# Two indirect transfers at a time: a wait ahead of each gather, add and store of a two-layer graph network

## The chip, the cores and the metric

One core of a Trainium2 chip runs the kernel. The metric is device time in microseconds, the median of several executions. Three executions of the kernel before took 1087.29, 1087.72 and 1098.17 us; the median is 1087.72 us. The profile is of one more execution.

## The reference

Input `x` has 32 batches of 512 nodes with 512 features, `adj` is a 512 x 512 matrix with few nonzero entries. Both layers normalise each row, take the positive part, mix and add the result to `x`:

```python
h = jnp.maximum(_layernorm(x, axis=-1), 0.0)
x = x + einsum(adj, h) @ weight + bias                 # layer 0: adj mixes the nodes
h = jnp.maximum(_layernorm(x, axis=-1), 0.0)
q, k, v = h @ Wq + bq, h @ Wk + bk, h @ Wv + bv        # layer 1: 8 heads
scores = q k^T / sqrt(64) + (1 - adj) * -1e9
x = x + softmax(scores) v @ Wo + bo
```

Where the penalty is so large that one neighbour takes the whole softmax, the attention of a row is a copy of one other row. The kernel establishes on the chip that this holds for its inputs, and then layer 1 is a product of the rows that are pointed at with `Wv Wo`, followed by a gather.

## The kernel before, in words

A prologue multiplies the weights, finds the neighbour of each row and decides on the path. `single_path` then handles one batch per round. Batches 0 to 4 run in the order of the input; beside them a `Plan` works out a new order of the nodes, in which the nonzero entries of `adj` fall into few blocks. From batch 5 (`FIRST`) on, `phase(range(FIRST, B + 1), True)` runs the regrouped loop (`sparse` is true), in which the rows of `x` are fetched and stored in the new order by indirect transfers. All indirect transfers are issued by GpSimd (POOL), one after the other, and their queue is q0 in the profile; plain transfers are issued by SyncE and go to q1.

A round `b` has 21 steps. `put(batch, step, f)` files a piece of work under a step; TensorE runs `layer0(b)` with steps 0 to 6, then `aggregate(b + 1)` (`spread`, L608 to L614) with steps 7 to 13, then `layer1(b - 1)` with steps 14 to 20. The order is written out by hand (`manual_schedule`); each engine runs its instructions in this order and waits on semaphores for data. The indirect transfers of a round, in POOL's order, each of 128 rows of 2 KB:

- `load_x(b + 2)`, step 0: four gathers of `x` into one of five buffers (`x<-in_x_dram,xi`, L462). A buffer is free once the stores of the batch before in it have landed.
- `load_g(b + 2)`, step 4: three gathers of extra rows into a single buffer (`at<-in_x_dram,gi`, L462). It is free once ScalarE has normalised the rows of the batch before out of it (`more_relu`, L933). ScalarE takes the statistics of the new rows in steps 13 to 18 (`more_stats`, L920).
- `finish(b - 2)`, step 7: four gathers that add the rows of layer 1 from memory onto `x` (`x<-z,pplace`, L462). They need the transfers `z<-zr` that SyncE issued after `put_z` (a transpose on VectorE, L718).
- `layer1` begins with a memset on POOL (L713) that clears the unused columns of `zs`. VectorE's transpose of `zs` in step 20 (`put_z`, L718) reads them.
- `store(b - 2)`, step 14: four scatters into the output (`out_dram<-x,xi`, L479), each followed by a small memset (L482).

In the first three rounds of the loop some of these are plain transfers or absent, since batches up to 5 are still in the input's order. The last rounds gather the last batches' layer 1 into buffers of their own (`fetch`, `get_all`).

Of the kernel before, what the change touches and what calls it, by code (L numbers as in the profile page):

```python
# [408 lines left out]
def single_path(ctx: ExitStack, tc: tile.TileContext, x, adj, out, kept, room):  # L409
    nc = tc.nc  # L410
    B, N, D = x.shape
# [28 lines left out]
    X, H0, PUT = {0: xs[0], 1: xs[1]}, {0: hs[0], 1: hs[1]}, {}  # L440
# [7 lines left out]
    def phase(batches, sparse):  # L448
        with ExitStack() as inner:
            small = inner.enter_context(tc.tile_pool(name="small", bufs=4))  # L450
            ps_m = inner.enter_context(tc.tile_pool(name="ps_m", bufs=6, space=PSUM))
            ps_t = inner.enter_context(tc.tile_pool(name="ps_t", bufs=2, space=PSUM))
            run_phase(batches, sparse, small, ps_m, ps_t)

    def run_phase(batches, sparse, small, ps_m, ps_t):
        ordered = folded and (sparse or batches[0] == 0)

        def natural(b):
            return not ordered or b <= FIRST

        def gather(dst, rows, at, **more):
            return nc.gpsimd.indirect_dma_start(out=dst, out_offset=None, in_=rows,  # L462
                                                in_offset=bass.IndirectOffsetOnAxis(ap=at, axis=0), **more)

        def load_x(b):
            X[b] = xs[b % 5]
            for c in range(C):
                if natural(b):
                    nc.sync.dma_start(X[b][:, c, :], x[b, c * P:(c + 1) * P, :])
                else:  # L470
                    gather(X[b][:, c, :], x_rows, plan.xi[:, b, c:c + 1])
# [3 lines left out]
        def store_rows(b, c, eng):  # L475
            if natural(b):
                eng.dma_start(out[b, c * P:(c + 1) * P, :], X[b][:, c, :])
                return
            stored = nc.gpsimd.indirect_dma_start(  # L479
                out=out_rows, out_offset=bass.IndirectOffsetOnAxis(ap=plan.xi[:, b, c:c + 1], axis=0),  # L480
                in_=X[b][:, c, :], in_offset=None)
            nc.gpsimd.memset(gap, 0.0)  # L482
            for other_rows in stored_rows:
                tc.declare_no_dep(stored.ins, other_rows.ins, reason="other rows")
            stored_rows.append(stored)

        def store(b):
            for c in range(C):
                store_rows(b, c, nc.sync)
# [84 lines left out]
        def look_up(table):  # L574
            for c in range(C):
                gather(place[:, c:c + 1], table, idx[:, c, 0:1])
# [44 lines left out]
        def load_g(b):  # L621
            for j in range(3):
                gather(plan.gx[:, j, :], x_rows, plan.gi[:, b, j:j + 1])
# [55 lines left out]
        def layer1_rows(b):  # L679
            for r in range(C):  # L680
                bank = ps_m.tile([P, D], F32, name="mm")
                for d in range(DC):
                    if d == 2 and r + 1 < C:
                        transpose_all(r + 1)
                    nc.tensor.matmul(bank, hs[1][:, d, r * P:(r + 1) * P], wvo[:, d, :], start=(d == 0),  # L685
                                     stop=(d == DC - 1))
                x_r = X[b][:, r, :].rearrange("p (q c e) -> p q c e", q=4, c=4)
                nc.vector.tensor_add(x_r, bank.rearrange("p (c q e) -> p q c e", q=4, c=4), x_r)
                store_rows(b, r, nc.sync)
                for i in range(2):  # L690
                    add_z(B - 3 + r // 2, 2 * (r % 2) + i, nc.sync if r < 2 else nc.scalar)
# [44 lines left out]
        def add_z(b, c, eng):  # L736
            nc.vector.tensor_add(X[b][:, c, :], late_z[b][:, c, :], X[b][:, c, :])
            store_rows(b, c, eng)
# [16 lines left out]
                                    pattern=[[1, P]], channel_multiplier=-1)  # L755
        last = []
        for b in batches:
            todo = [[] for _ in range(21)]

            def put(batch, step, f, *args):  # L760
# [805 lines left out]
```

## Time and profile before

| | before |
|---|---|
| median of the runs | 1087.72 us |
| profiled execution | 1089.15 us, span 1087.4 us |
| TensorE busy | 1011.2 us (93%) |
| VectorE busy | 810.1 us (74%) |
| ScalarE busy | 581.0 us (53%) |
| GpSimd busy | 564.2 us (52%) |
| indirect transfers of x: gathers, adds, stores | 104, 92, 104 |
| gathers of extra rows | 78 |
| time of the packets of q0 / q1, share of 16 engines | 45.4% / 30.0% |

A busy time on POOL is the time in which it makes a transfer's descriptors (1555 ns for an add, 948 to 1076 ns for the others), not the time until its data has landed. The page's list of DMA issues has no time to landing for indirect transfers; the chain of waits, and the semaphores' events, show some. An idle time stands before an instruction with what ended it: "issue" is none that the profile can name.

### The profile page before, as it was taken

What the parts mean: (1) busy time and instruction counts of PE and PEld (TensorE: products, weight loads), DVE (VectorE), ACT (ScalarE), POOL (GpSimd) and SP (SyncE); (2) the same over time, 40 slices, a digit from 0 to 9 for tenths busy, and PEclk for the clock granted to TensorE, in tenths of its full rate; (3) what the DMA queues carried; (4) which work ended last, traced back from release to release, by engine and by line L of the source; (5) the groups of instructions that cost most, each with busy time, mean ns of one, the idle gap of its engine ahead of it and who ended that gap; (6) DMA issues with size and microseconds to landing.
All of it is one profiled execution on the core that took longest, in us unless ns stands there. A gap on an engine that the chain in (4) does not pass through costs nothing.

```text
span 1087.4 us, 17059 instructions
## 1 busy us (share of the span) xinstructions
PE 1011.2 (93%) x5672; PEld 900.0 (83%) x5672; DVE 810.1 (74%) x1809; ACT 581.0 (53%) x1266; POOL 564.2 (52%) x659
## 2 busy tenths in 40 slices
PE   8999889978999889999999999999999998999993
PEld 7478778877898878999999988888889888999871
DVE  5897876857787658878777777778777776888762
ACT  3745345255555465566556556665555556666230
POOL 1023216646547435665575575555665565564326
PEclk9999999989899989999999999999999999999997
DMA  9244546968888768888888898988788787987654
GB/s 315 92 85 125 125 111 198 229 193 194 169 207 207 168 178 198 196 201 202 209 219 184 210 232 206 214 196 201 198 207 193 171 213 202 221 197 188 131 169 159
DMA packets 161314, 204.24 MB, mean 188 GB/s; under 512 B 17824, under 2 KB 105632, under 8 KB 161216
## 3 DMA queue, kind: packets, MB, share of 16 engines
q0 software_dynamic: 43984, 118.27, 45.4%
q1 hardware_dynamic: 115760, 83.37, 30.0%
q10 hardware_dynamic: 1472, 1.41, 0.4%
q8 instruction: 47, 0.77, 0.3%
q14 instruction: 51, 0.42, 0.1%
HBM read 120.66 MB, written 82.32 MB: 187 GB/s over the span
## 4 chain that ended last, share of the span: by engine, by line
PE 72%; ACT 4%; DVE 3%; issue 2%; POOL 2%; DMA 1%; another core or an unknown queue 1%; ACTq 0%; POOLq 0%; DVEq 0%
PE mm L495 51%; PE mm L611 11%; PE mm L614 6%; PE mm L608 2%; ACT zs L545 1%; POOL out_dram L479 1%; PE mm L685 1%; DVE st L361 1%; ACT h L379 1%; DMA x<-z,pplace 1%; DVE x L552 0%; DMA at<-in_x_dram,gi 0%; ACT h L394 0%; ACT yT L619 0%
## 5 line engine op out<-in xcount | busy, mean ns | idle before, releaser
L552 DVE TENSOR_TENSOR x<-mm,x 128x512 f32<-128x512 f32 x217 | 148.5, 685 | 130.2 <-PE mm L495 99.3
L379 ACT ACTIVATE h<-x,off,rstd 128x512 f32<-128x512 f32 x256 | 196.5, 807 | 7.8 <-DVE off L370 4.1
L365 ACT ACTIVATE rstd<-mv,eps 128x2 f32<-128x2 f32 (+1 forms) x91 | 26.6, 293 | 300.5 <-DVE mv L362 252.8
L495 PE MATMUL mm<-w_t,sel 128*128 128x256 f32 x744 | 176.1, 386 | 9.5 <-DVE x L552 9.4
L462 POOL DMA_INDIRECT x<-z,pplace x92 | 143.1, 1555 | 72.9 <-DMA z<-zr 37.4
L495 PEld LDWEIGHTS mm<-w_t,sel 128*128 128x128 f32 x744 | 142.1, 192 | 32.2 <-DVE x L552 12.7
L361 DVE BATCH_NORM_STATS2 st<-x 128x6 f32<-128x512 f32 x234 | 157.7, 674 | 1.1
L462 POOL DMA_INDIRECT at<-in_x_dram,gi x78 | 73.9, 948 | 162.0 <-ACT adjT L933 131.6
L495 PE MATMUL mm<-hTs,wvo_t 128*128 128x168 f32 x720 | 122.8, 317 | 32.3 <-ACT zs L545 31.0
L611 PE MATMUL mm<-ap,h 128*128 128x256 f32 x624 | 151.9, 380 | 0.0
L462 POOL DMA_INDIRECT x<-in_x_dram,xi x104 | 111.9, 1076 | 57.4 <-issue 27.1
L495 PEld LDWEIGHTS mm<-hTs,wvo_t 128*128 128x128 f32 x720 | 109.4, 196 | 38.6 <-ACT zs L545 37.3
L479 POOL DMA_INDIRECT out_dram<-x,xi x104 | 108.2, 1040 | 31.2 <-issue 22.0
L545 ACT ACTIVATE zs<-mm,cvo_c 128x168 f32<-128x168 f32 x240 | 82.8, 399 | 68.9 <-PE mm L495 50.9
L611 PEld LDWEIGHTS mm<-ap,h 128*128 128x128 f32 x624 | 110.6, 191 | 10.7
L495 PE MATMUL mm<-w_s,yT 128*128 128x256 f32 x496 | 118.5, 382 | 0.8 <-ACT zs L545 0.8
L495 PEld LDWEIGHTS mm<-w_s,yT 128*128 128x128 f32 x496 | 93.6, 192 | 12.7 <-ACT zs L545 1.0
L614 PEld LDWEIGHTS mm<-ag,adjT 128*128 128x128 f32 x624 | 86.0, 191 | 5.4
L614 PE MATMUL mm<-ag,adjT 128*128 128x128 f32 x624 | 86.4, 275 | 0.0
L586 DVE TENSOR_TENSOR x<-x,b_r 128x512 f32<-128x512 f32 x124 | 84.1, 679 | 0.0
L495 PE MATMUL mm<-hT,wvo 128*128 128x168 f32 x480 | 81.2, 314 | 0.0
L619 ACT COPY yT<-mm 128x512 f32<-128x512 f32 x104 | 59.8, 575 | 38.9 <-PE mm L614 30.3
(314 smaller groups left out, 1703.0 us busy)
## 6 DMA issues: line engine op xcount, KB each, us to landing
hc<-hs SPq DMA_DIRECT2D x124, 176.0 KB
z<-zr SPq DMA_DIRECT2D x120, 96.0 KB
z<-zr SPq DMA_DIRECT2D x120, 80.0 KB
hs<-h SPq DMA_DIRECT2D x50, 192.0 KB
hs<-h SPq DMA_DIRECT2D x50, 160.0 KB
out_dram<-x SPq DMA_DIRECT2D x24, 256.0 KB
x<-in_x_dram SPq DMA_DIRECT2D x16, 256.0 KB
x<-in_x_dram,xi POOLq DMA_INDIRECT x104
```

Source lines behind the costliest of these rows:

```text
L361: self.nc.vector.bn_stats(st, self.src[:, self.chunks[i], :])
L365: self.nc.scalar.activation(self.rstd[:, 0:len(self.chunks)], self.mv[:, :, 1], AF.Sqrt, bias=self.eps)
L379: self.nc.scalar.activation(dst, src, AF.Relu, bias=self.off[:, i:i + 1], scale=self.rstd[:, i:i + 1])
L462: return nc.gpsimd.indirect_dma_start(out=dst, out_offset=None, in_=rows, in_offset=bass.IndirectOffsetOnAxis(ap=at, axis=0), **more)
L479: stored = nc.gpsimd.indirect_dma_start(out=out_rows, out_offset=bass.IndirectOffsetOnAxis(ap=plan.xi[:, b, c:c + 1], axis=0), in_=X[b][:, ...
L495: nc.tensor.matmul(bank[:, m, 0:half], lhs[:, k, m * P:(m + 1) * P], rhs[:, k, :], start=(first and m == 0 and k == 0), stop=(k == 1), ski ...
L545: nc.scalar.activation(dst[:, m, :], bank[:, m, :], AF.Identity, bias=cvo_c[:, 2 * i + m:2 * i + m + 1])
L552: nc.vector.tensor_add(dst, bank, dst)
L586: nc.vector.tensor_add(X[b][:, c, :], X[b][:, c, :], b0_r)
L611: nc.tensor.matmul(two(bank, j), H0[b][:, j, cols], two(plan.ap[:, j, :], j), start=False, stop=False, skip_group_check=True)
L614: nc.tensor.matmul(bank[:, j * P:(j + 1) * P], extra[:, j - 1, cols], plan.ag[:, j - 1, j * P:(j + 1) * P], start=False, stop=(j == C - 1) ...
L619: nc.scalar.copy(yT[:, d, :], bank)
```

## The change

Each indirect transfer that `gather` and `store_rows` issue in the regrouped loop is passed through `paced`. It makes the transfer depend on the one issued two before it, as a dependence on data: POOL waits until that one has landed. `pacing[0]` turns this off for rounds 30 to 32. The transfers, their order and their data stay as they are.

```diff
+        moved, pacing = [], [True]
+
+        def paced(move):
+            if sparse and pacing[0]:
+                if len(moved) > 1:
+                    tc.add_manual_dep(move.ins, moved[-2].ins.name, mybir.DependencyInfo(
+                        mybir.DependencyClass.Sync, mybir.DependencyReason.DATA), reason="two at a time")
+                moved.append(move)
+            return move
+
         def gather(dst, rows, at, **more):
-            return nc.gpsimd.indirect_dma_start(out=dst, out_offset=None, in_=rows,
-                                                in_offset=bass.IndirectOffsetOnAxis(ap=at, axis=0), **more)
+            return paced(nc.gpsimd.indirect_dma_start(out=dst, out_offset=None, in_=rows,
+                                                      in_offset=bass.IndirectOffsetOnAxis(ap=at, axis=0), **more))
...
-            stored = nc.gpsimd.indirect_dma_start(
+            stored = paced(nc.gpsimd.indirect_dma_start(
                 out=out_rows, out_offset=bass.IndirectOffsetOnAxis(ap=plan.xi[:, b, c:c + 1], axis=0),
-                in_=X[b][:, c, :], in_offset=None)
+                in_=X[b][:, c, :], in_offset=None))
...
         for b in batches:
+            pacing[0] = b < B - 2
             todo = [[] for _ in range(21)]
```

## The prediction

> **What bounds the kernel now.** I read the busy shares on the page first, then the chain that ended last, then the waits inside the regrouped loop (412 to 984 us), then one round of that loop on the timeline.
>
> ```profile
> PE 1011.2 (93%) x5672; PEld 900.0 (83%) x5672; DVE 810.1 (74%) x1809; ACT 581.0 (53%) x1266; POOL 564.2 (52%) x659
> ...
> q0 software_dynamic: 43984, 118.27, 45.4%
> ...
> PE 72%; ACT 4%; DVE 3%; issue 2%; POOL 2%; DMA 1%; another core or an unknown queue 1%; ACTq 0%; POOLq 0%; DVEq 0%
> ```
>
> TensorE sets the pace: 93% busy, 72% of the chain. POOL, which issues every indirect transfer (queue q0), is half idle, and DMA is 1% of the chain. The waits of POOL in the loop (who waits for whom: us in total, times, longest) say why it is idle:
>
> ```profile
> POOL at L462 <- ACT adjT L933: 98.8, 21, 9.2
> ...
> POOL x L462 <- DMA z<-zr: 26.7, 10, 4.0
> ...
> POOL x L462 <- DMA out_dram<-x,xi: 13.6, 14, 2.1
> ```
>
> POOL mostly waits for ScalarE to have read the previous batch's extra rows (98.8 us): it has arrived early and is held by the data. In the same stretch no wait of TensorE, VectorE or ScalarE worth listing is for a DMA. One round (start, us, engine, line, what, idle before it and who ended it):
>
> ```profile
> 762.36 0.95 POOL L462 DMA_INDIRECT at<-in_x_dram,gi  x1 [7.09 <-ACT adjT L933]
> ...
> 767.79 1.59 POOL L462 DMA_INDIRECT x<-z,pplace  x1 [1.65 <-DMA z<-zr]
> 769.68 1.55 POOL L462 DMA_INDIRECT x<-z,pplace  x1 [0.30 <-issue]
> ...
> 774.35 0.73 POOL L713 MEMSET zs<- 128x64 f32 x1
> ...
> 775.25 1.04 POOL L479 DMA_INDIRECT out_dram<-x,xi  x1 [0.17 <-issue]
> ...
> 779.61 0.63 ACT L920 ACTIVATE adjT<-at 128x512 f32<-128x512 f32 x1
> ...
> 784.51 0.95 POOL L462 DMA_INDIRECT x<-in_x_dram,xi  x1 [0.57 <-DMA out_dram<-x,xi]
> ...
> 788.75 0.84 DVE L718 STREAM_TRANSPOSE zr<-zs 128x640 f32<-128x640 f32 x1
> ...
> 792.40 0.96 POOL L462 DMA_INDIRECT at<-in_x_dram,gi  x1 [5.69 <-ACT adjT L933]
> ```
>
> A round is 15 indirect transfers: 3 gathers of extra rows (762.36 on), 4 adds of z into x (767.79 on), 4 stores (775.25 on), 4 gathers of x (781.06 on). An issue holds POOL about 1 us (add 1.55), the next follows 0.3 us later, and POOL never waits for a landing unless data asks for it. The landing comes much later than the next issue. The chain of waits gives two, from issue to landing:
>
> ```profile
> 212.63 4.86 DMA at<-in_x_dram,gi
> ...
> 441.70 5.44 DMA x<-z,pplace
> ```
>
> So with an issue every 1.3 to 1.9 us, three or four transfers are under way inside a burst. The first gathers of extra rows of the loop start at 403.77 and 974.98, 19 rounds apart: 30.06 us a round.
>
> **The change, part by part.** Nothing is removed: the same transfers in the same order. Added is one wait ahead of each of the 15 issues, for the landing of the last but one. POOL's queue is in order, so everything behind waits too: the other transfers, the 0.11 us memsets after stores (nobody waits for them) and the memset of zs, L713. Of that one VectorE's transpose at L718 (788.75) is a reader, and ScalarE's statistics at L920 (779.61) need the gathered extra rows.
>
> The rate of the new queue follows from the landings. Two chains of transfers run beside each other, each advancing by one landing plus the start after it; a round of 15 costs half the sum of their times. Start after landing: 0.26 us (the x gather at 784.51 starts 0.26 us after the semaphore's event; other waits for one semaphore give 0.26 too, for several 0.77 to 0.85). Times from start to the last recorded increment of the transfer's semaphore, sorted by how many earlier ones were still under way, from the trace's semaphore events:
> - gathers of extra rows: 3.6 with none ahead (median of 13), mean 4.35 with none or one (40), 4.55 with more. Gathers of x: the same bytes the same way, 5.4 with one to three ahead.
> - adds: 4.9 with none, 5.0 with none or one (25), 5.2 with more.
> - stores: 3.8 with one ahead (only two), 4.85 with more; the early scatters hs<-h, which also write 128 rows to memory, 2.7.
>
> Paced, exactly one is ahead. I take 4.35 for all seven gathers, 5.0 for the adds, 3.8 for the stores: (7 x 4.35 + 4 x 5.0 + 4 x 3.8 + 15 x 0.26) / 2 = 69.6 / 2 = **34.8 us a round** against 30.06. Low end, with the lowest rows: (7 x 3.6 + 4 x 4.9 + 4 x 2.7 + 3.9) / 2 = 29.8. High end, with the present crowd's times, since the hardware queue's 30% stays and may be what stretches them: (4 x 5.4 + 3 x 4.55 + 4 x 5.2 + 4 x 4.85 + 3.9) / 2 = 39.7. I stay in the middle because the rows with none or one ahead are nearest to the new state.
>
> The Trainium skill (DMA: Bandwidth & Descriptors, "Anatomy of one DMA") speaks against a loss: it puts a transfer from this engine at 2.0 us plus bytes over 436 GB/s, so 2.6 us for 256 KB. An estimate from that page with the trace's issue and start times added, 15 x (2.6 + 1.16 + 0.26) / 2 = 30.2 us a round, would hide the change altogether. The landings recorded here are 3.6 us at best and 5 us as a rule, so I go by the rows.
>
> What covers the lateness, and for how long: POOL's idle time ahead of the extra rows. In the paced queue the memset of zs ends (3 x 4.35 + 3 x 5.0 + 6 x 0.26) / 2 + 1.55 + 0.73 = 17.1 us after the first gather of extra rows; L718 reads it 788.75 - 762.36 = 26.4 us after that gather. So POOL may be 9.3 us late before VectorE stands; then the put of z, the adds behind it on VectorE, the PSUM banks and TensorE stand. The extra rows for L920 have 779.61 - 762.36 - 4.35 = 12.9 us and come second. The loads of x have more. After two rounds that cover is gone, and each further round costs all of 4.7 us.
>
> Sum: 19 x (34.8 - 30.06) - 9.3 = 80.8 us. The rounds before 403.77 add nothing: those at 342 and 376 took 33.7 and 36.4 us anyway with a clock of 0.95 and 0.91, and the earlier ones have 7 to 11 paced transfers. From batch 30 pacing is off, so the tail stays. Profiled execution 1089.15 + 80.8 = 1170; the median shown is 1.4 lower: **1168 us**.
>
> **Rivals.**
> - *Hidden.* With two under way landings come down to the lowest rows and a round stays under 30.06 + 9.3/19 = 30.55 us. For it: q0 has less to queue for. Against it: every row must be at its minimum at once, and a late landing holds two issues. 1088 us.
> - *Faster.* Hidden as above, and the hardware queue, no longer sharing the engines with three or four gathers, lets TensorE run through: between 412 and 984 TensorE is idle 572.0 - 554.1 = 17.9 us. If all of it went: 1070 us. It decides only under 30.55 us a round. Against it: those gaps end on ScalarE's zs and VectorE's x, not on a DMA.
> - *Harsher.* Landings stay at the crowd's times, or each issue pays 0.77 us for two semaphores: rounds of 37.3 to 39.7 us, 19 x 7.2 - 9.3 = 128 to 19 x 9.6 - 9.3 = 173 us more: 1216 to 1261.
> - *No change in fact:* the wait is implied by one already there. Each transfer already waits for the one eight before it (it reuses its semaphore), which is no such limit. 1088.
>
> **How the numbers follow.** The queue as the bound, 32.3 to 37.3 us a round: 0.71, 1168 us, its own range 1120 to 1216. Harsher 0.12, hidden 0.09, no change in fact 0.03, faster 0.05. The range of 8 in 10 leaves out the faster case and the upper part of the harsher one, and reaches down nearly to the hidden one: 1095 to 1225. Faster by over 1% (about what a measurement can tell from no change): 0.05. Within: 0.12. Slower: 0.83.
>
> **What would show it.** In the changed profile: POOL's wait for ScalarE (L933) gone and waits of POOL for DMA (x, at, out_dram) of 1 to 3 us at nearly each issue; rounds of some 35 us from the third or fourth paced round of 15 on; VectorE waiting for the memset L713 or ScalarE for the extra rows; TensorE's share down to about 87%; q0's packets no shorter than 10%. Times from issue to landing near 4.4, 5.0 and 3.8 us. The prediction is wrong if landings with one ahead are under 3.7 us for gathers, or if POOL still waits for L933.

## The result, and the profile after

| | before | after |
|---|---|---|
| median of the runs | 1087.51 us (1085.68 to 1098.17) | 1198.34 us (1195.41 to 1199.71) |
| profiled execution | 1089.15 us, span 1087.4 us | 1195.41 us, span 1193.6 us |
| first gather of extra rows of the loop's 19 rounds, first / last | 403.8 / 975.0 us | 415.3 / 1087.1 us |
| one round | 30.06 us | 35.36 us |

The kernel is slower: ratio 1.0993, 95% interval [1.0919, 1.1068]. That is 2.6% above the forecast of 1168 us and inside its range. In the tables and texts below a line number of after is 10 or 11 higher than that of before: the gathers are L472, the stores L489, the memset of `zs` L723, the transpose in `put_z` L728, the products L505.

The page of after, its busy shares, the queue of the indirect transfers (packets, MB, share of 16 engines' span) and the chain that ended last:

```profile
PE 1048.0 (88%) x5672; PEld 920.6 (77%) x5672; DVE 804.4 (67%) x1809; ACT 578.4 (48%) x1266; POOL 561.2 (47%) x659
...
q0 software_dynamic: 43984, 118.27, 41.2%
...
DMA 36%; PE 18%; DVE 12%; POOL 9%; issue 8%; ACT 3%; SPq 0%; POOLq 0%; another core or an unknown queue 0%; ACTq 0%; DVEq 0%
```

TensorE's 72% of the chain have become 18%, and the DMA's 1% has become 36%: the end is now set by landings. No engine has more instructions; POOL is busy for 561 us of 1194 and is the bound all the same, because it stands and waits. The queue's packets took as long as before in total (41.2% of 1193.6 us is 492 us, 45.4% of 1087.4 us was 494 us).

The waits of after over the whole span (who waits for whom: us in total, times, longest):

```profile
DVE zr L728 <- POOL zs L723: 116.9, 23, 6.5
PEld mm L505 <- DVE x L562: 104.9, 28, 5.7
PE mm L505 <- DVE x L562: 93.6, 26, 5.3
...
POOL x L472 <- DMA x<-z,pplace: 79.0, 40, 3.9
POOL x L472 <- DMA out_dram<-x,xi: 56.6, 24, 3.0
POOL out_dram L489 <- DMA x<-z,pplace: 52.6, 35, 4.0
...
POOL x L472 <- DMA x<-in_x_dram,xi: 49.3, 37, 5.0
```

Read from below: POOL waits for landings at transfers that depend on nothing else there (an add for an add, a store for an add, a gather for a store). Then the first row: VectorE waits for the memset of `zs`, 23 times for 5.1 us. Then TensorE waits for VectorE's `x`, because the additions that empty its PSUM banks stand behind that transpose. POOL's wait for ScalarE to free the extra rows, 131.6 us over the whole span before, is no longer among them.

One round of POOL (start, us, engine, line, what, in brackets the idle time before it and who ended it):

```profile
778.15 1.59 POOL L472 DMA_INDIRECT x<-z,pplace  x1 [1.95 <-DMA at<-in_x_dram,gi]
780.05 1.55 POOL L472 DMA_INDIRECT x<-z,pplace  x1 [0.31 <-issue]
784.75 1.53 POOL L472 DMA_INDIRECT x<-z,pplace  x1 [3.14 <-DMA x<-z,pplace]
786.93 1.53 POOL L472 DMA_INDIRECT x<-z,pplace  x1 [0.65 <-DMA x<-z,pplace]
787.90 0.73 POOL L723 MEMSET zs<- 128x64 f32 x1
789.85 1.03 POOL L489 DMA_INDIRECT out_dram<-x,xi  x1 [1.22 <-DMA x<-z,pplace]
...
793.38 0.96 POOL L489 DMA_INDIRECT out_dram<-x,xi  x1 [0.19 <-issue]
794.64 0.96 POOL L489 DMA_INDIRECT out_dram<-x,xi  x1 [0.19 <-issue]
...
797.43 0.98 POOL L472 DMA_INDIRECT x<-in_x_dram,xi  x1 [1.72 <-DMA out_dram<-x,xi]
```

The third and fourth add wait for the first and second; the memset of `zs` can't pass them. The third and fourth store (793.38, 794.64) don't wait, although the change asks for it, so 13 of a round's 15 transfers wait and not all: more on this in the experiments. The chain through the same place shows how the wait reaches TensorE (start, us, what):

```profile
780.05 6.62 DMA x<-z,pplace
786.67 0.26 issue
786.93 1.53 POOL x L472
788.46 0.18 POOL zs L723
...
788.66 0.85 DVE zr L728
...
789.83 0.98 DVE zr L728
790.81 0.59 DVE x L562
791.40 0.04 issue
791.44 8.72 PE mm L505 x32
```

The second add lands after 6.62 us, the fourth is issued, the memset runs, VectorE transposes twice and adds, and only then has TensorE a bank to write into.

The balance is made from three differences. At the loop's first gather of extra rows after is 415.3 - 403.8 = 11.5 us late, from the rounds before. The 19 rounds add 19 x (35.36 - 30.06) = 100.7 us. From there to the end of the span it is 1193.6 - 1087.1 = 106.5 us where it was 112.4 us, so 5.9 us come back. The sum is 106.3 us; the spans differ by 106.2.

### The profile page after: what moved, and what is told of

Same layout as the page of the kernel before. It is cut to its first block, busy times and chain, and to the rows that moved or that the text cites. A ratio compares the mean times of both kernels' runs of the same rounds, so it can differ in the third digit from the quotient of the medians.

```text
span 1193.6 us, 17085 instructions
## 1 busy us (share of the span) xinstructions
PE 1048.0 (88%) x5672; PEld 920.6 (77%) x5672; DVE 804.4 (67%) x1809; ACT 578.4 (48%) x1266; POOL 561.2 (47%) x659
## 3 DMA queue, kind: packets, MB, share of 16 engines
q0 software_dynamic: 43984, 118.27, 41.2%
## 4 chain that ended last, share of the span: by engine, by line
DMA 36%; PE 18%; DVE 12%; POOL 9%; issue 8%; ACT 3%; SPq 0%; POOLq 0%; another core or an unknown queue 0%; ACTq 0%; DVEq 0%
PE mm L505 17%; DMA x<-z,pplace 15%; DMA at<-in_x_dram,gi 12%; POOL x L472 5%; DMA x<-in_x_dram,xi 4%; DVE st L361 3%; DVE x L562 2%; DVE zr L728 2%; POOL out_dram L489 2%; ACT h L379 2%; DMA out_dram<-x,xi 2%; DMA x<-z,place 1%; DVE hT L715 1%; DVE mv L362 1%; DMA z<-zr 1%
## 5 line engine op out<-in xcount | busy, mean ns | idle before, releaser
L505 PE MATMUL mm<-w_t,sel 128*128 128x256 f32 x744 | 209.2, 432 | 94.0 <-DVE x L562 93.6
L505 PEld LDWEIGHTS mm<-w_t,sel 128*128 128x128 f32 x744 | 157.8, 216 | 129.9 <-DVE x L562 104.4
L472 POOL DMA_INDIRECT x<-z,pplace x92 | 153.6, 1670 | 124.5 <-DMA x<-z,pplace 79.0
L472 POOL DMA_INDIRECT x<-in_x_dram,xi x104 | 100.7, 968 | 122.6 <-DMA out_dram<-x,xi 56.6
L489 POOL DMA_INDIRECT out_dram<-x,xi x104 | 103.2, 992 | 66.1 <-DMA x<-z,pplace 52.6
L728 DVE STREAM_TRANSPOSE zr<-zs 128x640 f32<-128x640 f32 (+1 forms) x60 | 54.7, 912 | 117.9 <-POOL zs L723 116.9
L505 PE MATMUL mm<-hTs,wvo_t 128*128 128x168 f32 x720 | 116.5, 310 | 14.7 <-ACT zs L555 13.0
L505 PE MATMUL mm<-w_s,yT 128*128 128x256 f32 x496 | 128.7, 406 | 0.8 <-ACT zs L555 0.8
L472 POOL DMA_INDIRECT at<-in_x_dram,gi x78 | 76.3, 979 | 108.7 <-ACT h L379 27.5
L505 PEld LDWEIGHTS mm<-hTs,wvo_t 128*128 128x128 f32 x720 | 106.0, 191 | 18.1 <-ACT zs L555 16.2
L505 PEld LDWEIGHTS mm<-w_s,yT 128*128 128x128 f32 x496 | 102.9, 211 | 17.2 <-ACT zs L555 1.0
L505 PE MATMUL mm<-hT,wvo 128*128 128x168 f32 x480 | 79.2, 309 | 0.0
```

Source lines behind the costliest of these rows:

```text
L472: return paced(nc.gpsimd.indirect_dma_start(out=dst, out_offset=None, in_=rows, in_offset=bass.IndirectOffsetOnAxis(ap=at, axis=0), **more))
L489: stored = paced(nc.gpsimd.indirect_dma_start(out=out_rows, out_offset=bass.IndirectOffsetOnAxis(ap=plan.xi[:, b, c:c + 1], axis=0), in_=X ...
L505: nc.tensor.matmul(bank[:, m, 0:half], lhs[:, k, m * P:(m + 1) * P], rhs[:, k, :], start=(first and m == 0 and k == 0), stop=(k == 1), ski ...
L728: nc.vector.transpose(zr[:, s0:s1, :].rearrange("p s (c e) -> p s c e", c=4), zt(b)[:, :, 32 * s0:32 * s1].rearrange("p c (s j) -> p s c j ...
```

## The experiments

All ratios are to the kernel before, run beside on the same chip; its median there was 1070.5 to 1083.7 us on three chips, so ratios and not times are compared. Rounds are taken as in the table above, from the first gathers of extra rows of the loop's 19 rounds, in one profiled execution of each kernel.

**How many may be under way.** The theory is a rate: the round is the sum of landings and starts over the limit, or TensorE's own round where that is longer. The rival is a price per added wait.

`e2_one` lets one be under way:

```diff
-                if len(moved) > 1:
-                    tc.add_manual_dep(move.ins, moved[-2].ins.name, mybir.DependencyInfo(
+                if len(moved) > 0:
+                    tc.add_manual_dep(move.ins, moved[-1].ins.name, mybir.DependencyInfo(
```

> Each indirect transfer waits for the one just before it (stores among themselves still do not). Theory (rate): a round is the sum of what now runs in pairs: gathers 7 x 3.8, adds 4 x 5.6, stores about 8, two-semaphore starts 2: 56 to 60 us a round, 1600 to 1780 us in all. Rival (cost per wait): as many waits as in the changed kernel: 1180 to 1230 us.

Measured: 1734.9 us in one execution, 57.6 us a round. The rate holds; a price per wait would have changed little, since there are nearly as many waits (12 a round for 13). With none ahead landings are 3.3 to 4.1 us for gathers and 4.8 to 5.0 for adds; the stores, three of which don't wait for the store before, take 2.8 to 3.4. Its row in the waits is the same as that of after, longer:

```profile
DVE zr L728 <- POOL zs L723: 390.0, 24, 19.0
```

`e1_three` lets three be under way, with `len(moved) > 2` and `moved[-3]`.

> Each indirect transfer waits for the last but two instead of the last but one: as many waits as in the changed kernel, a looser limit. Theory (the limit sets a rate, and the rate of POOL's queue sets the round): a round's landings and starts add up to about 71 us, or 79 us with landings stretched to those of three under way, so a third of that, 24 to 26 us a round, is under the 30.06 us of the kernel before; the loss is gone: 1080 to 1100 us, VectorE's wait for the memset of zs under 10 us. Rival (every added wait costs some time of its own, as a pause of POOL or of the queue): the 13 waits a round are still there, so most of the 110 us stays: 1150 to 1200 us.

Measured: 1058.12 us, ratio 0.9799 [0.9731, 0.9867]. The loss is gone, and more than was expected: it is faster than the kernel before. `e10_three_again` is the same kernel on another chip, and `e9_three_all` gives the fourth store of a round the wait for the first that the change leaves out there as well:

> The limit of three once more, on the chip of the other two runs. If the gain belongs to the limit: ratio 0.973 to 0.987, no idle time of TensorE ahead of layer 1's products. If it was the chip's: ratio 0.995 to 1.005.

> At most three under way, for every transfer (the fourth store of a round waits for the first as well). Rate theory: with three under way a round is TensorE's, 28.9 to 29.5 us, and the one added wait is met long before it matters: ratio 0.975 to 0.99 to the kernel before. Rival (the gain of the limit of three was the chip's and not the limit's): ratio 0.995 to 1.005.

Measured: 0.9831 [0.9726, 0.9935] and 0.9887 [0.9778, 0.9997]. Rounds took 28.94, 28.91 and 29.14 us in the three. The gain, 1.1 to 2.0% by the three ratios, belongs to the limit of three and not to a chip. The page of `e10_three_again`, busy shares and chain:

```profile
PE 1004.5 (95%) x5672; PEld 896.5 (85%) x5672; DVE 808.6 (77%) x1809; ACT 578.8 (55%) x1266; POOL 566.5 (54%) x659
...
PE 72%; DVE 5%; issue 3%; ACT 2%; POOL 2%; DMA 1%; SPq 0%; ACTq 0%; POOLq 0%; DVEq 0%
```

TensorE is the bound again, at 95%. In 412 to 940 us its waits come to 1.3 us, and these are all:

```profile
PE mm L505 <- DVE x L562: 1.0, 1, 1.0
PE mm L505 <- issue: 0.3, 1, 0.3
```

The kernel before had 17.9 us of idle time in its loop. What went with the limit of three is mostly that idle time: the 19 rounds are 19 x (30.06 - 28.91) = 21.9 us shorter, of which 16.6 us are idle time of TensorE (17.9 to 1.3 us) and 5.3 us its busy time (553.3 to 548.0 us).

`e7_four` lets four be under way, with `len(moved) > 3` and `moved[-4]`.

> At most four under way. Theory (rate): about 79 us of landings and starts over 4, some 20 us a round: no loss by the rate, ratio to before at or under 1.00. Theory T (timing of the gathers of x): they are held less than with three, by about 1 us a round, and part of the idle time at layer1 is back: ratio 0.98 to 1.00. Theory N (number): between before and three: 0.985 to 0.995. Rival (cost per wait): 1.05 to 1.10.

Measured: ratio 0.9974 [0.9922, 1.0027], no difference from before; 29.45 us a round, TensorE idle 6.6 us in 412 to 940. That is in the range of theory T and above that of theory N. That three is better than four is clear only against `e1_three`: the intervals of the two other runs of three overlap this one.

| under way | round, us | ratio of time | TensorE's mean clock |
|---|---|---|---|
| 1 | 57.6 | one execution, 1734.9 us | 0.806 |
| 2 (after) | 35.36 | 1.0993 | 0.947 |
| 3 | 28.94 / 28.91 | 0.9799 / 0.9831 | 0.983 |
| 4 | 29.45 | 0.9974 | 0.980 |
| no limit (before) | 30.06 | 1 | 0.979 |

The waits made in a round were 12, 13, 14 and 15 for the limits of one to four, so a price per added wait is excluded: 12 waits cost most and 15 nothing.

**Which of the waits.** `e5_gathers` limits the seven gathers of a round alone, among themselves (an add is the one that passes `more`):

```diff
         def gather(dst, rows, at, **more):
-            return paced(nc.gpsimd.indirect_dma_start(out=dst, out_offset=None, in_=rows,
-                                                      in_offset=bass.IndirectOffsetOnAxis(ap=at, axis=0), **more))
+            move = nc.gpsimd.indirect_dma_start(out=dst, out_offset=None, in_=rows,
+                                                in_offset=bass.IndirectOffsetOnAxis(ap=at, axis=0), **more)
+            return move if more else paced(move)
...
-            stored = paced(nc.gpsimd.indirect_dma_start(
+            stored = (nc.gpsimd.indirect_dma_start(
```

`e6_adds_stores` limits the adds and stores alone: the stores stay as in after, and the last line of `gather` is

```diff
+            return paced(move) if more else move
```

> The limit of two holds for the gathers of x and of the extra rows alone, counted among themselves; adds and stores go as in the kernel before. Theory (rate): the seven gathers take about 15 us of POOL's round in place of 9, adds and stores about 13 as before: some 28 us, just under 30.06: 1085 to 1105 us. Rival (cost per wait): 7 of 13 waits are there, about 57 us of 110: 1130 to 1155 us.

> The limit of two holds for the adds and the stores alone, counted among themselves; gathers go as in the kernel before. Theory (rate): adds and stores take about 17 to 20 us of POOL's round in place of 13, the gathers about 9: 27 to 29 us, under 30.06: 1085 to 1105 us. Rival (cost per wait): 6 of 13 waits are there, about 50 us: 1125 to 1150 us.

Measured: 0.9941 [0.9901, 0.9980] and 1.0199 [1.0111, 1.0287], with rounds of 30.08 and 31.16 us. The halves bring 0.6% and cost 2.0%; together they cost 9.9%. So it is not a sum of waits. With the gathers alone VectorE does wait for the memset, but the round stays at that of before:

```profile
DVE zr L729 <- POOL zs L724: 30.4, 17, 3.0
```

What the 2% of the adds and stores consist of is not settled: POOL still waits for ScalarE to free the extra rows there (57.8 us), so the queue was not the bound in each round, and TensorE's idle time of 28.6 us lies mostly ahead of the layer 0 products (22.5 us). The profile is of the longest of its four executions, 1113.45 us, where the median is 1103.6; the round of 31.16 us is from it too.

**The stores that don't wait.** `store_rows` declares each store independent of the earlier stores of its batch, after `paced` has added its dependence, and this takes the added one away too. So 13 of 15 transfers wait. `e4_stores_wait` leaves the added dependence in:

```diff
-            for other_rows in stored_rows:
+            for other_rows in stored_rows[:-2] + stored_rows[-1:]:
                 tc.declare_no_dep(stored.ins, other_rows.ins, reason="other rows")
```

> The changed kernel, with the waits that it lacks: a store's dependence on the store two before it is declared away together with the order among stores, so the third and the fourth store of a round start 0.2 us after the one before without a wait. Here they wait too. Theory (rate, from the landings in the changed kernel's trace): third and fourth store 0.6 and 1.3 us later, but landing sooner, and the two gathers of x behind them wait for one semaphore in place of two: about even, 34.9 to 35.7 us a round, ratio to before 1.085 to 1.12. Rival (four stores together are what keeps the loss down): 37 us a round and more, ratio above 1.13.

Measured: 1195.46 us, ratio 1.115 [1.1046, 1.1254], 34.96 us a round. The third and fourth store now start 0.27 us after the landing of the last but one, and no difference from after can be told: its round is 0.4 us shorter, its ratio is not lower, and the intervals overlap. The slip of the change has no weight in the result.

**The place where the lateness comes out.** `e3_memset_once` keeps the limit of two and makes the memset of `zs` only in the first rounds of each buffer (and in the last but one); the columns stay clear afterwards.

```diff
-            if room < 32 * S:
+            if room < 32 * S and (b < 2 or b == B - 2):
```

> The changed kernel without the memset of zs on POOL in each round (its columns are cleared in the first rounds and nothing else writes them). Theory (the rate of POOL's queue sets the round, the memset is only the first place where the lateness shows): the slope of 35.4 us a round stays; the next reader that stands is ScalarE at the statistics of the extra rows, which comes 3.6 us later, once: 1185 to 1199 us, VectorE's wait of 117 us gone and a wait of ScalarE for the extra rows of 80 to 120 us in its place. Rival (the memset behind the waits is what costs, since it alone holds VectorE): back to 1085 to 1110 us.

Measured: 1210.96 us, ratio 1.1204 [1.1122, 1.1285]. Its waits, in the same form as those of after:

```profile
ACT adjT L931 <- DMA at<-in_x_dram,gi: 118.3, 25, 9.1
PE mm L505 <- ACT zs L555: 113.4, 26, 7.7
...
DVE st L361 <- DMA x<-in_x_dram,xi: 64.9, 54, 3.5
```

VectorE's wait for the memset is gone, and ScalarE's statistics wait for the extra rows in its place (118.3 us for 116.9), with TensorE behind ScalarE. The memset is where the queue's lateness shows, not what costs. The time did not fall by the expected few microseconds; by the ratio it rose by some 2%, though the kernel before beside it had 1079.2 us, and beside after 1087.5 (`e4_stores_wait`, close to after, had a ratio of 1.115 beside 1070.5). The round of 36.45 us can be taken apart: summed landings of the 15 transfers 64.0 us (64.6 in after), and summed starts after the landing of the last but one 8.7 us (6.0 in after). The adds start 0.72 to 0.74 us after that landing here and 0.26 us in after. Half of 2.7 us, less half of the 0.6 us, is the 1.1 us that the round is longer. The traces show what goes with the later start: all 76 adds of the 19 rounds wait for a second semaphore here, that of VectorE, which in after none of them does and the memset ahead of the stores does. Starts after two semaphores took longer in after as well, 0.76 us for the gathers of extra rows. So in after the memset's wait for VectorE seems to cover that of the adds behind it.

**Why three is faster than no limit.** In the kernel before, TensorE's idle time stood almost wholly (17.0 of 17.9 us, 15 times, in 11 of the 19 rounds) ahead of layer 1's third product (11 times) and fifth (4 times). One such place on the timeline of before, with other instructions left out:

```profile
749.18 1.31 PE L495 MATMUL mm<-hT,wvo 128*128 128x168 f32 x8
...
749.66 0.99 POOL L462 DMA_INDIRECT x<-in_x_dram,xi  x1 [0.19 <-issue]
...
750.48 0.59 ACT L619 COPY yT<-mm 128x512 f32<-128x512 f32 x1
...
751.94 0.69 ACT L545 ACTIVATE zs<-mm,cvo_c 128x168 f32<-128x168 f32 x2 [0.87 <-PE mm L495]
...
752.69 1.41 PE L495 MATMUL mm<-hTs,wvo_t 128*128 128x168 f32 x8 [1.06 <-ACT zs L545]
```

By the record (in which the ends of matmuls are modelled) the product is done at 750.49, ScalarE is free at 751.07 and still waits for it until 751.94. Such a delay of 0.5 to 3 us came in rounds in which a gather of `x` is issued within some 1.5 us of that product; with only stores nearby it was 0.04 us. It does not come each time: the product that ended at 935.60 had gathers 0.5 us before and 0.8 us after its end, and a delay of 0.04 us. In the limit of three (`e10_three_again`) the first of those gathers comes 4.3 us or more after that product. `e8_late_x` asks whether their place alone does it: it is the kernel before, with the first gather of `x` of a round held until ScalarE has taken layer 1's third product (`third` holds that activation, of the piece `u2`).

```diff
-                    gather(X[b][:, c, :], x_rows, plan.xi[:, b, c:c + 1])
+                    move = gather(X[b][:, c, :], x_rows, plan.xi[:, b, c:c + 1])
+                    if c == 0 and third:
+                        tc.add_manual_dep(move.ins, third[-1].ins.name, mybir.DependencyInfo(
+                            mybir.DependencyClass.Sync, mybir.DependencyReason.DATA), reason="later")
```

> The kernel before, without any limit on how many are under way; added is one wait a round: the first gather of x waits until ScalarE has evacuated the third product of layer1, about 3.5 us after layer1's start. It asks why the limit of three was faster than the kernel before (ratio 0.98). In the trace of before TensorE idles 17 us at layer1's first products, in rounds in which a gather of x is issued within about 1.5 us of them; in that of three under way the gathers of x come later and TensorE idles 1.3 us. Theory T (the time at which the gathers of x start is what disturbs): ratio to before 0.975 to 0.985, TensorE's gaps at layer1 gone. Theory N (the number of transfers under way is what disturbs): no gain, 0.995 to 1.005, the gaps stay.

Measured: ratio 0.9977 [0.9926, 1.0027]. Each expectation was half met: the idle time at layer 1 went, by the place of the gathers alone, but the time did not go with it. TensorE had 10.2 us of idle time at another place, ahead of layer 0's products. The trace shows that ScalarE's delay did not go either, it followed the gathers: in 14 of the 18 rounds in 412 to 945 us ScalarE took layer 1's last product 0.3 to 2.2 us later than its end and ScalarE's own work allowed, with gathers of `x` issued 1 to 2.5 us before that end. In `e10_three_again` the gathers come as near to the last product, and it was so in 5 rounds. `e11_late_again` is the same kernel beside `e10_three_again`:

> The kernel before with the first gather of x held until layer 1's third product is evacuated, once more, beside the limit of three. If the place of the gathers alone made the limit of three faster: the same ratio as the limit of three within 0.007. If the number under way matters beyond the place: 0.99 to 1.00, and TensorE idle 8 to 12 us in the loop.

Measured: 1.0039 [0.9990, 1.0089], against 0.9831 for the limit of three on that chip: not the place of the gathers alone. The idle time of TensorE, 17.2 us, was above both expectations' figures. TensorE's waits in 412 to 940 us of `e11_late_again`:

```profile
PE mm L498 <- DVE x L557: 15.6, 14, 2.1
PE mm L498 <- ACT zs L548: 1.6, 4, 0.5
```

Moving the gathers moves the delay and the idle time and removes neither. That the limit of three removes it is shown; by which mechanism is open. The place of the gathers is not the whole of it.

## Why the prediction was right

- **The queue becomes the bound, at the sum of landings and starts over two: right.** Predicted 34.8 us a round, measured 35.36. That it came so near is partly luck: the parts were off in both directions. Summed landings were taken as 65.7 us and were 64.6: the seven gathers had 3.68 us on average and not 4.35, the four adds 5.80 and not 5.0 (the second of them 6.78), the stores 3.92 for 3.8. Summed starts were taken as 15 x 0.26 = 3.9 us and were 6.0: the gathers of extra rows start 0.76 us after the landing, not 0.26. The harsher rival had that price for every transfer. Over 19 rounds the difference of 0.56 us is 10.6 us. Landings and starts, counted from the landing two before, add up to twice the round in any kernel; what makes them an account is that the starts stayed at mostly 0.26 to 0.9 us, so that nothing but the landings held the queue.
- **A sign of being wrong that came.** The prediction called itself wrong "if landings with one ahead are under 3.7 us for gathers". The seven gathers had 3.68 us, those of `x` 3.40. The queue was the bound even so, because the adds and the starts took more than foretold; the sign watched one term of the sum alone.
- **"The rounds before 403.77 add nothing": wrong, 11.5 us.** I argued that those rounds were slow anyway or had few paced transfers. The round that begins at 274.1 us took 39.4 us where it was 31.0 us. It has 11 paced transfers, but landings there are far above the rows of the loop: the gather issued at 278.10 took 9.9 us and the add behind it 9.5 us, and in the kernel before the seven at this place took 9.5 to 11.0 us, one beside the other. With two under way such landings are waited for one after the other: in 230 to 415 us of after POOL waited up to 7.0 us for a gather of extra rows to land and up to 5.0 us for one of `x` (12.3 and 16.4 us in all) before it could issue the next transfer.
- **The cover of 9.3 us and "the tail stays": right in kind, too large.** 5.9 us came back after the last round, 3.4 less than I took off; how much of it is cover and how much a shorter tail is not separated. With 10.6 and 11.5 that is the 25.5 us by which the 106.3 us measured exceed the 80.8 predicted.
- **VectorE's transpose first, ScalarE's statistics second: right,** the first in after (116.9 us), the second in `e3_memset_once` (118.3 us).
- **Signs in the profile.** TensorE's share (87% foretold, 88% found), POOL's wait for ScalarE gone, q0's packet time unchanged: as foretold. (Rows of after still name ScalarE ahead of the gathers of extra rows, 27.5 and 18.7 us, but these start 0.8 us after the landing of the last but one, as others that wait for two semaphores do.) "1 to 3 us at nearly each issue" was too much: the waits alternate, one long and the next short, and two of the stores have none.
- **Rivals.** Hidden and no change in fact are excluded by the ratio, harsher by the rounds. *Faster* is excluded for a limit of two, but its price, all of the 17.9 us of TensorE's idle time, is most of what the limit of three gained in the loop. I had written against it that those gaps end on ScalarE and not on a DMA. That was no reason: they still go away when fewer transfers are under way.
- **The Trainium skill's figure.** The page "DMA: Bandwidth & Descriptors", section "Anatomy of one DMA", gave an estimate of 30.2 us a round, which would have been hidden; in it are 15 x (2.6 + 1.16) = 56.4 us of landings. With two under way the measurement decides against it: 64.6 us of landings and 6.0 us of starts. With one under way landings were 57.2 us (`e2_one`), close to the estimate. I had set its 2.6 us, without the issue, beside landings with the issue in them; what it lacks here is not the single transfer but what a second one under way adds.

## What to carry to other kernels

A limit on transfers under way sets a rate: add up the landings and starts of a round, divide by the limit and compare with the round of the engine that is the bound. Here that is 35 us against 30 for two. For three an estimate from the landings of `e1_three` and the starts of after is (73.4 + 6.0) / 3 = 26.5 us, under TensorE's own round. So two was a loss of 10% and three a gain of 1 to 2%; one step of the limit decides the sign, so it has to be swept and not guessed. When an instruction that others need stands in the same in-order queue behind such a wait, it shows as the culprit in the list of waits, and taking it out only hands the wait to the next reader.

## What the runs showed of the hardware

- **Landings grow with what else is under way, the packets' time does not.** The summed landings of a round's 15 transfers were 75.7 us with no limit, 64.6 us with two under way and 57.2 us with one. The time of q0's packets on the engines was the same in all: 494, 492 and 497 us (28.7% of 1733.1 us in `e2_one`). So what is added to a landing is not slower packets but time ahead of them or between them. The stores show it most, 5.2 us on average before, 3.9 us with two, 3.1 us with one; the adds don't follow, with 5.1, 5.8 and 4.9 us. That the number under way in q0 is the cause is not shown: stores with two others ahead took 4.5 us before and 3.0 us in `e2_one`, and the busy share of the DMA engines in the 19 rounds fell with the limit as well (0.85, 0.70 and 0.44).
- **TensorE's clock drops after a long stall.** After the 4.28 us of idle time ahead of 791.44 us the granted clock was 0.82 for the next 8.8 us and 1.00 after that; by the trace's record of the clock it was one half from 791.17 to 794.58 us. In the 19 rounds of after TensorE stood 19 times for over 2 us: at the 17 stalls of 3.7 to 5.3 us the clock was one half for 3.4 or 6.8 us, at those of 2.6 and 3.0 us it stayed. The windows of after (window; us; busy time of each engine; PEclk, DMA share, GB/s):

```profile
791.40:800.20 8.80, 8.76 (x33) 7.47 (x34) 3.29 (x6) 3.46 (x5) 4.23 (x7) 0.82 0.76 223
800.20:812.00 11.80, 11.80 (x75) 11.00 (x74) 11.38 (x30) 6.33 (x13) 5.61 (x6) 1.00 0.55 153
```

So a bound elsewhere makes TensorE's busy time longer, 1048.0 us for 1011.2, with the same 5672 matmuls. In the 19 rounds it is 589.5 us for 553.3, more than a third of the 100.7 us that they are longer. The Trainium skill (TensorE: Matmul & The Clock Gate, "Part 1: The HAM clock gate") has half the clock after an idle window of about 3.4 us, until it has been busy for about as long. An estimate from that page, 3.4 us at half speed within 8.8 us, makes a mean of 0.81; the trace has 0.82.

- **ScalarE can take a product late,** by 0.3 to 3 us after its recorded end, when indirect gathers are issued near it. The traces show the coincidence, that it does not come each time, and that the delay moves with the gathers (`e8_late_x`); they don't show the path.
